# Inverse standard deviation as a power on GpSimd, weight splits on GpSimd alone, the first block normalised tile by tile

## The chip, the cores and the metric

The kernel runs on one core of one Trainium2 chip. The metric is the device time in microseconds of one launch. TensorE (PE in the profile), VectorE (DVE), ScalarE (ACT), GpSimd (POOL) and SyncE (SP) each have an instruction queue of their own and work in the order of that queue.

## The reference

One layer of a transformer-like model: a layernorm, then a time-mixing recurrence and a feed-forward network (FFN) side by side, and a residual sum. x is 4 x 1024 x 512 in float32, HIDDEN is 704, N is 2048.

```python
xn = _layernorm(x, axis=-1)                      # no gain, no bias, eps 1e-5
# attention branch
xx = jnp.concatenate([xn[:, 1:2, :], xn[:, :-1, :]], axis=1) - xn
k = jnp.einsum('btc,hc->bth', xn + xx * time_mix_k, Wk)
r = jnp.einsum('btc,hc->bth', xn + xx * time_mix_r, Wr)
w = jnp.exp(-jnp.exp(time_decay))
# over t: state = state * w + relu(k_t);  o_t = state * r_t
a = jnp.einsum('bth,ch->btc', o, Wv)
a = (a - mean(a)) * rsqrt(var(a) + EPS) * ln_gamma + ln_beta
# ffn branch
D = gelu(float16(xn) @ W0.T + bias0).astype(float16)
E = (D @ W1.T + bias1).astype(float16)
return x + a + E
```

## The kernel before

The 4 x 1024 rows are cut into eight blocks of 512 rows (TB), and a block into four tiles of 128 rows (s = 0 to 3), with the rows in the partitions. The 512 channels make four chunks of 128 (c), the 704 hidden units six chunks (h, the last one of 64), the 2048 inner units of the FFN sixteen (n).

For each block the work is this:

- `layernorm` takes mean and variance of each tile (`stats_of`, L169 and L170, on DVE), makes the inverse standard deviation of all four tiles at once (`rstd_of`: a square root on ACT at L163, a reciprocal on DVE at L164), and normalises each tile in place (`normalize`, L173, on DVE).
- `mixed_inputs` turns the tiles by TensorE transposes (L196) into PSUM tiles `pt`, one per c, from which ACT makes `xnT` in float32 (L199) and `x16` in float16 (L203). DVE forms the shifted difference `xx` (L209) and the two mixed inputs `xk` and `xnT` (L211). POOL saves the last column for the next block (`last`, L206, and L190).
- `attention` makes for each h the product `pk` (L229), its ReLU `rk` on ACT (L237), the recurrence `st` as a scan on DVE (L239), the product `pr` (L251) and `g` = `st` x `pr` on DVE (L258). POOL keeps the last column of `st` as `carry` (L248). `st` has two buffers, `rk` one, and `pk` and `pr` share two PSUM buffers with `pd`.
- `ffn` makes for each n the product `pd` (L300), its GELU in float16 on ACT (L308), a cast `d` back on DVE (L310), and adds the product of `d` with the second weights to four PSUM tiles `pe` (L316). In the text n counts the steps of this loop.
- Between steps of `ffn` other stages are called: at n = 1 `out_stage`, which is `attention_out`; at n = 6 the layernorm of the next block; at n = 10 its `mixed_inputs`. `attention_out` makes `po` (L269), copies it to `z` (L277, ACT), normalises it with its own statistics `mvy` and `ry`, multiplies by gamma and adds beta on POOL (L285, L286), and adds the reloaded x on DVE (L287). The statistics of the next block are `mvx` and `rx`.
- `finish` adds `pe`, the bias and `z` (L337, L338) and stores the tile.

FFN weights are held as two parts that TensorE multiplies one after the other: `split` rounds the loaded tile `raw` to a high part (L121, on ACT) and subtracts it to get a low part (L122, on POOL). W0 is split in sixteen tiles of 128x512 into `w0h` and `w0l`; they are loaded after the attention of block 0 in program order. W1 is split in sixteen tiles in the FFN of block 0, one per n, and written to DRAM (L143), from where the other blocks load it (L145). `raw` has three buffers. All these loads are issued from SP's queue, each once its buffer is free.

The order in which the functions are written is not the order in the queues. A planner orders each engine's instructions by what it thinks is ready, with the program order as priority. So the statistics of the next block are found on DVE directly behind those of `po`, though they are called five steps later.

Of the kernel before, what the change touches and what calls it, by code (L numbers as in the profile page):

```python
# [9 lines left out]
F32 = mybir.dt.float32  # L10
F32R = mybir.dt.float32r
AF = mybir.ActivationFunctionType
ALU = mybir.AluOpType

P = 128
EPS = 1e-5
# [3 lines left out]
def time_mix_and_gelu_ffn(  # L20
# [26 lines left out]
    nc = tc.nc  # L47
# [3 lines left out]
    TB = 512  # L51
    NS = TB // P
    NC = C // P
# [6 lines left out]
    def pool(name, bufs, **kw):  # L60
        return ctx.enter_context(tc.tile_pool(name=name, bufs=bufs, **kw))

    const = pool("const", 1)
    one = pool("one", 1)
    two = pool("two", 2)
    three = pool("three", 3)
    four = pool("four", 4)
    ps_mm = pool("ps_mm", 2, space=bass.MemoryType.PSUM)
    ps_e = pool("ps_e", 4, space=bass.MemoryType.PSUM)
    ps_t = pool("ps_t", 2, space=bass.MemoryType.PSUM)  # L70
    dram = pool("dram", 1, space=bass.MemoryType.DRAM)

    def load_x(i):
        b, t0 = blocks[i]
        tiles = []
        for s in range(NS):
            t = four.tile([P, C], F32, tag="x", name=f"x_{i}_{s}")
            nc.sync.dma_start(t, x[b, t0 + s * P : t0 + (s + 1) * P, :])
            tiles.append(t)
        return tiles  # L80


    x_now = load_x(0)
    ident = const.tile([P, P], F32, name="ident")
    make_identity(nc, ident)
    eps_sb = const.tile([P, 1], F32, name="eps_sb")
    nc.vector.memset(eps_sb, EPS)

    mk_sb = const.tile([P, NC], F32, name="mk_sb")
    mr_sb = const.tile([P, NC], F32, name="mr_sb")  # L90
# [27 lines left out]
    b1_sb = const.tile([P, C], F32, name="b1_sb")  # L118

    def split(hi, lo, raw):  # L120
        nc.scalar.copy(hi, raw)  # L121
        nc.gpsimd.tensor_sub(lo, raw, hi.bitcast(F32))  # L122

    W0G = 512
# [32 lines left out]
    last = const.tile([P, NC, 1], F32, name="last")  # L157
    carry = const.tile([P, NH], F32, name="carry")

    def rstd_of(mv, name):  # L160

        r = two.tile([P, NS], F32, tag="rstd", name=name)
        nc.scalar.activation(r, mv[:, :, 1], AF.Sqrt, bias=eps_sb)  # L163
        nc.vector.reciprocal(r, r)  # L164
        return r

    def stats_of(mv, s, src, name):
        st6 = two.tile([P, 6], F32, tag="st6", name=name)
        nc.vector.bn_stats(st6, src)  # L169
        nc.vector.bn_aggr(mv[:, s, :], st6)  # L170

    def normalize(dst, src, mv, s, rstd):
        nc.vector.tensor_scalar(  # L173
            dst, src, mv[:, s, 0:1], rstd[:, s : s + 1], ALU.subtract, ALU.mult
        )

    def layernorm(i, xs):

        mv = two.tile([P, NS, 2], F32, tag="mv", name=f"mvx_{i}")
        for s in range(NS):  # L180
            stats_of(mv, s, xs[s], f"stx_{i}_{s}")
        rstd = rstd_of(mv, f"rx_{i}")
        for s in range(NS):
            normalize(xs[s], xs[s], mv, s, rstd)

    def mixed_inputs(i, xn):

        t0 = blocks[i][1]
        if t0 > 0:
            nc.gpsimd.tensor_copy(xnT[:, :, 0:1], last)  # L190
        x16s = []
        xk = one.tile([P, NC, TB], F32, tag="xk", name=f"xk_{i}")
        for c in range(NC):
            pt = ps_t.tile([P, TB], F32, tag="pt", name=f"pt_{i}_{c}")
            for s in range(NS):
                nc.tensor.transpose(  # L196
                    pt[:, s * P : (s + 1) * P], xn[s][:, c * P : (c + 1) * P], ident
                )
            nc.scalar.copy(xnT[:, c, 1:], pt)  # L199
            if t0 == 0:  # L200
                nc.vector.tensor_copy(xnT[:, c, 0:1], pt[:, 1:2])
            x16 = four.tile([P, TB], F16, tag="x16", name=f"x16_{i}_{c}")
            nc.scalar.copy(x16, pt)  # L203
            x16s.append(x16)
            if t0 + TB < T:
                nc.gpsimd.tensor_copy(last[:, c, :], xnT[:, c, TB : TB + 1])  # L206
            xx = two.tile([P, TB], F32, tag="xx", name=f"xx_{i}_{c}")
            now = xnT[:, c, 1:]
            nc.vector.tensor_sub(xx, xnT[:, c, :TB], now)  # L209
            for dst, m in ((xk[:, c, :], mk_sb), (now, mr_sb)):  # L210
                nc.vector.scalar_tensor_tensor(  # L211
                    dst, xx, m[:, c : c + 1], now, ALU.mult, ALU.add
                )
        return x16s, xk

    def ffn_input(i, x16s):
        xf = one.tile([P, NC, TB], F32R, tag="xf", name=f"xf_{i}")
        for c in range(NC):
            nc.vector.tensor_copy(xf[:, c, :], x16s[c])
        return xf  # L220

    def attention(i, xk):

        b, t0 = blocks[i]
        g = one.tile([P, NH, TB], F32, tag="g", name=f"g_{i}")
        for h, (h0, hw) in enumerate(hid):
            pk = ps_mm.tile([P, TB], F32, tag="mm", name=f"pk_{i}_{h}")
            for c in range(NC):
                nc.tensor.matmul(  # L229
                    pk[:hw],  # L230
                    wk_sb[c][:, h0 : h0 + hw],
                    xk[:, c, :],
                    start=(c == 0),
                    stop=(c == NC - 1),
                )
            rk = two.tile([P, TB], F32, tag="rk", name=f"rk_{i}_{h}", bufs=1)
            nc.scalar.activation(rk[:hw], pk[:hw], AF.Relu)  # L237
            st = two.tile([P, TB], F32, tag="st", name=f"st_{i}_{h}")
            nc.vector.tensor_tensor_scan(  # L239
                st[:hw],  # L240
                w_sb[:hw, h : h + 1].to_broadcast([hw, TB]),
                rk[:hw],
                0.0 if t0 == 0 else carry[:hw, h : h + 1],
                ALU.mult,
                ALU.add,
            )
            if t0 + TB < T:
                nc.gpsimd.tensor_copy(carry[:hw, h : h + 1], st[:hw, TB - 1 : TB])  # L248
            pr = ps_mm.tile([P, TB], F32, tag="mm", name=f"pr_{i}_{h}")
            for c in range(NC):  # L250
                nc.tensor.matmul(  # L251
                    pr[:hw],
                    wr_sb[c][:, h0 : h0 + hw],
                    xnT[:, c, 1:],
                    start=(c == 0),
                    stop=(c == NC - 1),
                )
            nc.vector.tensor_mul(g[:hw, h, :], st[:hw], pr[:hw])  # L258
        return g

    def attention_out(i, g):

        b, t0 = blocks[i]
        zs = []
        mv = two.tile([P, NS, 2], F32, tag="mv", name=f"mvy_{i}")
        for s in range(NS):
            po = ps_t.tile([P, C], F32, tag="pt", name=f"po_{i}_{s}")
            for h, (h0, hw) in enumerate(hid):
                nc.tensor.matmul(  # L269
                    po,  # L270
                    g[:hw, h, s * P : (s + 1) * P],
                    wv_sb[:hw, h, :],
                    start=(h == 0),
                    stop=(h == NH - 1),
                )
            z = four.tile([P, C], F32, tag="z", name=f"z_{i}_{s}")
            nc.scalar.copy(z, po)  # L277
            stats_of(mv, s, z, f"sty_{i}_{s}")
            zs.append(z)
        rstd = rstd_of(mv, f"ry_{i}")  # L280
        for s in range(NS):
            xr = two.tile([P, C], F32, tag="xres", name=f"xres_{i}_{s}")
            nc.sync.dma_start(xr, x[b, t0 + s * P : t0 + (s + 1) * P, :])
            normalize(zs[s], zs[s], mv, s, rstd)
            nc.gpsimd.tensor_mul(zs[s], zs[s], gamma_sb)  # L285
            nc.gpsimd.tensor_add(zs[s], zs[s], beta_sb)  # L286
            nc.vector.tensor_add(zs[s], xr, zs[s])  # L287
        return zs
# [44 lines left out]
    def finish(i, zs, pe):  # L333
        b, t0 = blocks[i]
        for s in range(NS):
# [2 lines left out]
            nc.vector.tensor_add(zs[s], zs[s], e16)  # L338
            nc.sync.dma_start(out[b, t0 + s * P : t0 + (s + 1) * P, :], zs[s])

    layernorm(0, x_now)
    x16s, xk = mixed_inputs(0, x_now)
    xf = ffn_input(0, x16s)
    for i in range(len(blocks)):
        more = i + 1 < len(blocks)
        state = {}
        g = attention(i, xk)
        if i == 0:
            for grp in range(N // W0G):
                load_w0(grp)  # L350
            load_late_constants()
        if more:
            x_now = load_x(i + 1)

        def out_stage():
            state["zs"] = attention_out(i, g)

        def next_norm():
            layernorm(i + 1, x_now)

        def next_inputs():
            state["mixed"] = mixed_inputs(i + 1, x_now)

        between = {1: out_stage}
        if more:
            between[6] = next_norm
            between[10] = next_inputs
        pe = ffn(i, xf, between)
        if more:
            x16s, xk = state["mixed"]  # L370
            xf = ffn_input(i + 1, x16s)
        finish(i, state["zs"], pe)
# [43 lines left out]
```

## Time and profile before

| | |
|---|---|
| Time, three runs | 1095.02, 1095.55 and 1097.2 us; median 1095.55 |
| The profiled execution | 1094.07 us, of which the span is 1092.1 us |
| Busy: PE, DVE, ACT, POOL | 1026.3, 430.5, 216.5 and 152.8 us |
| Granted TensorE clock, mean | 0.975 of full speed |
| Block 0 | attention from 16.6 us, FFN from 69.5, end about 162.7 |
| Blocks 1 to 6 | 131.4 to 132.0 us each |
| Block 7, with the end | 138 us |

The table gives whole times; what the prediction rests on are rows of the profile. A row of a group gives a line, an engine, an operation, the tile written and the tiles read, and the count; then its busy time and the mean of one in ns; then how long the engine stood idle just before, and what ended the wait. A row of the timeline gives start and duration in us, and the idle time before it in brackets. Busy time of a matmul is modelled, and a matmul at half clock counts as busy.

### The profile page before, as it was taken

The page shows a single profiled execution, that of the slowest core. Times are in us where ns is not written, and L with a number is a line of the kernel's source. Part 1 is how long each engine was busy: PE and PEld are TensorE (multiplying, and loading weights), DVE is VectorE, ACT ScalarE, POOL GpSimd, SP SyncE. Part 2 cuts the span into 40 slices and gives each one's busy share as a digit, 9 for nine tenths or more (in the row PEclk, how much of TensorE's full clock was granted, in tenths as well). Part 3 has the DMA queues.
Part 4 walks back from the last instruction along what each step waited for, and adds up shares of the span by engine and source line. Part 5 has one row for each costly group of instructions (what it writes and reads, how often), then busy time and mean ns, then how long its engine had stood idle before and what let it go on. Part 6 is the DMA issues. An engine that isn't in the chain of part 4 may idle for free.

```text
span 1092.1 us, 8897 instructions
## 1 busy us (share of the span) xinstructions
PE 1026.3 (94%) x3328; PEld 614.0 (56%) x3328; DVE 430.5 (39%) x674; ACT 216.5 (20%) x341; POOL 152.8 (14%) x146
## 2 busy tenths in 40 slices
PE   5899899989999899998999989999899998999997
PEld 2344674447744486445864467544685446744476
DVE  7324453243621625217342163421634225342332
ACT  4312230121201231012310123011230111301211
POOL 3612520031000400004000040000400003000210
PEclk9999899999999899998999989999899998999999
DMA  7730652004600145002540034400443014420043
GB/s 229 247 107 30 208 194 60 19 30 164 205 7 20 58 163 184 1 19 89 171 145 1 20 115 157 133 0 20 135 161 108 1 34 140 131 81 19 20 154 116
DMA packets 43147, 106.37 MB, mean 97 GB/s; under 512 B 8224, under 2 KB 8224, under 8 KB 43104
## 3 DMA queue, kind: packets, MB, share of 16 engines
q1 hardware_dynamic: 39248, 105.79, 29.2%
q10 hardware_dynamic: 3856, 0.02, 0.2%
q8 instruction: 26, 0.43, 0.2%
q14 instruction: 17, 0.14, 0.0%
HBM read 89.01 MB, written 16.78 MB: 97 GB/s over the span
## 4 chain that ended last, share of the span: by engine, by line
PE 54%; issue 31%; DVE 7%; DMA 3%; POOL 3%; ACT 1%; SPq 0%; ACTq 0%; DVEq 0%; POOLq 0%
PE pe L316 19%; PE pd L300 16%; PE pk L229 8%; PE pr L251 6%; PE po L269 4%; DVE z L287 2%; POOL z L285 2%; PE pt L196 1%; DMA out<-z 1%; DVE d L310 1%; DMA w0raw<-in_L_ffn_W 1%; POOL z L286 1%; DVE z L173 1%; POOL w0l L122 1%; DVE e L337 1%
## 5 line engine op out<-in xcount | busy, mean ns | idle before, releaser
L316 PE MATMUL pe<-w,d 128*128 128x512 f32 x1024 | 268.2, 407 | 41.2 <-DVE d L310 41.2
L316 PEld LDWEIGHTS pe<-w,d 128*128 128x128 f32 x1024 | 198.2, 195 | 93.1 <-DVE d L310 47.0
L300 PE MATMUL pd<-xf,w0h 128*128 128x512 f32 x512 | 207.5, 405 | 0.0
L300 PE MATMUL pd<-xf,w0l 128*128 128x512 f32 x512 | 204.1, 399 | 0.0
L229 PE MATMUL pk<-xk,wk 128*128 128x512 f32 (+1 forms) x384 | 177.8, 606 | 4.0 <-ACT rk L237 3.9
L269 PE MATMUL po<-wv_sb,g 128*128 128x512 f32 (+1 forms) x384 | 177.2, 607 | 0.0
L251 PE MATMUL pr<-xnT,wr 128*128 128x512 f32 (+1 forms) x384 | 174.4, 595 | 1.2 <-DVE g L258 0.9
L308 ACT ACTIVATE d<-pd,b_sb 128x512 f16<-128x512 f32 x128 | 88.3, 690 | 344.6 <-PE pd L300 340.0
L310 DVE CAST d<-d 128x512 fp32r<-128x512 f16 x128 | 64.3, 504 | 224.8 <-ACT d L308 224.3
L285 POOL TENSOR_TENSOR z<-z,gamma_sb 128x512 f32<-128x512 f32 x32 | 50.8, 1606 | 545.6 <-DVE z L173 545.6
L269 PEld LDWEIGHTS po<-wv_sb,g 128*128 128x128 f32 (+1 forms) x384 | 68.2, 189 | 104.0 <-issue 103.2
L229 PEld LDWEIGHTS pk<-xk,wk 128*128 128x128 f32 (+1 forms) x384 | 70.2, 185 | 100.3 <-issue 93.6
L251 PEld LDWEIGHTS pr<-xnT,wr 128*128 128x128 f32 (+1 forms) x384 | 69.4, 181 | 98.6 <-issue 94.7
L300 PEld LDWEIGHTS pd<-xf,w0h 128*128 128x128 f32 x512 | 98.2, 192 | 34.3 <-issue 12.6
L300 PEld LDWEIGHTS pd<-xf,w0l 128*128 128x128 f32 x512 | 97.8, 191 | 22.4
L169 DVE BATCH_NORM_STATS2 sty<-z 128x6 f32<-128x512 f32 x32 | 22.2, 695 | 164.4 <-ACT z L277 164.4
L237 ACT ACTIVATE rk<-pk 128x512 f32<-128x512 f32 (+1 forms) x48 | 28.6, 596 | 280.2 <-PE pk L229 280.2
L239 DVE TENSOR_TENSOR_SCAN st<-w_sb,rk 128x512 f32<-128x512 f32 (+1 forms) x24 | 31.4, 1308 | 77.4 <-ACT rk L237 77.4
L258 DVE TENSOR_TENSOR g<-st,pr 128x512 f32<-128x512 f32 (+1 forms) x48 | 32.9, 686 | 68.5 <-PE pr L251 68.2
L239 DVE TENSOR_TENSOR_SCAN st<-w_sb,carry,rk 128x512 f32<-128x512 f32 (+1 forms) x24 | 30.8, 1283 | 70.2 <-ACT rk L237 70.2
L277 ACT COPY z<-po 128x512 f32<-128x512 f32 x32 | 18.8, 586 | 168.3 <-PE po L269 168.3
L286 POOL TENSOR_TENSOR z<-z,beta_sb 128x512 f32<-128x512 f32 x32 | 44.6, 1414 | 0.0
(41 smaller groups left out, 449.7 us busy)
## 6 DMA issues: line engine op xcount, KB each, us to landing
w<-w1d SPq DMA_DIRECT2D x112, 512.0 KB, 3.3
x<-in_L_attn_x SPq DMA_DIRECT2D x32, 256.0 KB, 3.9
xres<-in_L_attn_x SPq DMA_DIRECT2D x32, 256.0 KB, 2.7
w1d<-w SPq DMA_DIRECT2D x16, 512.0 KB, 2.9
out<-z SPq DMA_DIRECT2D x32, 256.0 KB, 4.4
w0raw<-in_L_ffn_W SPq DMA_DIRECT2D x16, 256.0 KB, 3.7
w1raw<-in_L_ffn_W SPq DMA_DIRECT2D x16, 256.0 KB, 3.5
wk<-in_L_attn_Wk SPq DMA_DIRECT2D x4, 352.0 KB, 4.5
```

The source lines that it names most:

```text
L229: nc.tensor.matmul(pk[:hw], wk_sb[c][:, h0 : h0 + hw], xk[:, c, :], start=(c == 0), stop=(c == NC - 1),)
L237: nc.scalar.activation(rk[:hw], pk[:hw], AF.Relu)
L239: nc.vector.tensor_tensor_scan(st[:hw], w_sb[:hw, h : h + 1].to_broadcast([hw, TB]), rk[:hw], 0.0 if t0 == 0 else carry[:hw, h : h + 1], A ...
L251: nc.tensor.matmul(pr[:hw], wr_sb[c][:, h0 : h0 + hw], xnT[:, c, 1:], start=(c == 0), stop=(c == NC - 1),)
L258: nc.vector.tensor_mul(g[:hw, h, :], st[:hw], pr[:hw])
L269: nc.tensor.matmul(po, g[:hw, h, s * P : (s + 1) * P], wv_sb[:hw, h, :], start=(h == 0), stop=(h == NH - 1),)
L285: nc.gpsimd.tensor_mul(zs[s], zs[s], gamma_sb)
L286: nc.gpsimd.tensor_add(zs[s], zs[s], beta_sb)
L300: nc.tensor.matmul(pd, w[c][:, cols], xf[:, c, :], start=(c == 0 and w is w0h), stop=(c == NC - 1 and w is w0l),)
L308: nc.scalar.activation(d16, pd, AF.Gelu, bias=b0_sb[:, n : n + 1])
L310: nc.vector.tensor_copy(d, d16)
L316: nc.tensor.matmul(pe[s], d[:, s * P : (s + 1) * P], w1[:, part, :], start=(n == 0 and part == 0), stop=(n == NN - 1 and part == 1),)
```

## The change

It has four parts.

- `rstd_of` now works on POOL: it adds eps to the variance and raises the sum to the power -0.5 with a constant tile `nhalf`. The square root on ACT and the reciprocal on DVE are gone, and with them the constant `eps_sb`. This holds for the layernorm of each block and for that of `po`.
- `split` makes both parts on POOL; the rounding copy was on ACT.
- The first block goes tile by tile: statistics, `rstd_of` for a single column, normalise, and four transposes, before the next tile. It uses four PSUM tiles of the pool that `pe` has later. The other blocks keep the old order (`transposed`).
- `mixed_inputs` takes the transposed tiles as an argument.

```diff
-    eps_sb = const.tile([P, 1], F32, name="eps_sb")
-    nc.vector.memset(eps_sb, EPS)
+    nhalf = const.tile([P, NS], F32, name="nhalf")
+    nc.vector.memset(nhalf, -0.5)
...
     def split(hi, lo, raw):
-        nc.scalar.copy(hi, raw)
+        nc.gpsimd.tensor_copy(hi, raw)
         nc.gpsimd.tensor_sub(lo, raw, hi.bitcast(F32))
...
-    def rstd_of(mv, name):
+    def rstd_of(var, name):
-        r = two.tile([P, NS], F32, tag="rstd", name=name)
-        nc.scalar.activation(r, mv[:, :, 1], AF.Sqrt, bias=eps_sb)
-        nc.vector.reciprocal(r, r)
+        n = var.shape[1]
+        r = two.tile([P, n], F32, tag=f"rstd{n}", name=name)
+        nc.gpsimd.tensor_scalar_add(r, var, EPS)
+        nc.gpsimd.tensor_tensor(r, r, nhalf[:, :n], ALU.pow)
         return r
...
+    def first_transposed(xs):
+        pts = [ps_e.tile([P, TB], F32, tag="pe", name=f"pt_0_{c}") for c in range(NC)]
+        for s in range(NS):
+            mv = four.tile([P, 1, 2], F32, tag="mv0", name=f"mvx_0_{s}")
+            stats_of(mv, 0, xs[s], f"stx_0_{s}")
+            rstd = rstd_of(mv[:, :, 1], f"rx_0_{s}")
+            normalize(xs[s], xs[s], mv[:, 0, 0:1], rstd)
+            for c in range(NC):
+                nc.tensor.transpose(
+                    pts[c][:, s * P : (s + 1) * P], xs[s][:, c * P : (c + 1) * P], ident
+                )
+        return pts
...
-    layernorm(0, x_now)
-    x16s, xk = mixed_inputs(0, x_now)
+    x16s, xk = mixed_inputs(0, first_transposed(x_now))
```

More of the change, by code (lines that the diff above doesn't have):

```diff
@@ L170, in stats_of, with normalize @@
         nc.vector.bn_aggr(mv[:, s, :], st6)
[L172 to L175, printed above, removed]
+    def normalize(dst, src, mean, rstd):
+        nc.vector.tensor_scalar(dst, src, mean, rstd, ALU.subtract, ALU.mult)
     def layernorm(i, xs):
@@ L181, in layernorm, with transposed @@
             stats_of(mv, s, xs[s], f"stx_{i}_{s}")
-        rstd = rstd_of(mv, f"rx_{i}")
+        rstd = rstd_of(mv[:, :, 1], f"rx_{i}")
         for s in range(NS):
[L184 to L192, printed above, removed]
+            normalize(xs[s], xs[s], mv[:, s, 0:1], rstd[:, s : s + 1])
+    def transposed(i, xn):
         for c in range(NC):
@@ L198, in mixed_inputs @@
                 )
+            yield pt
+    def first_transposed(xs):
[10 more added lines that the diff above has]
+        return pts
+    def mixed_inputs(i, pts):
+        t0 = blocks[i][1]
+        if t0 > 0:
+            nc.gpsimd.tensor_copy(xnT[:, :, 0:1], last)
+        x16s = []
+        xk = one.tile([P, NC, TB], F32, tag="xk", name=f"xk_{i}")
+        for c, pt in enumerate(pts):
             nc.scalar.copy(xnT[:, c, 1:], pt)
@@ L279, in attention_out @@
             zs.append(z)
-        rstd = rstd_of(mv, f"ry_{i}")
+        rstd = rstd_of(mv[:, :, 1], f"ry_{i}")
         for s in range(NS):
@@ L283, in attention_out @@
             nc.sync.dma_start(xr, x[b, t0 + s * P : t0 + (s + 1) * P, :])
-            normalize(zs[s], zs[s], mv, s, rstd)
+            normalize(zs[s], zs[s], mv[:, s, 0:1], rstd[:, s : s + 1])
             nc.gpsimd.tensor_mul(zs[s], zs[s], gamma_sb)
@@ L361, in next_inputs @@
         def next_inputs():
-            state["mixed"] = mixed_inputs(i + 1, x_now)
+            state["mixed"] = mixed_inputs(i + 1, transposed(i + 1, x_now))
         between = {1: out_stage}
```

## The prediction

> **What bounds the kernel now.** The first view read is the page: busy time by engine, then the groups of instructions with what ended the idle time before them.
>
> ```profile
> PE 1026.3 (94%) x3328; PEld 614.0 (56%) x3328; DVE 430.5 (39%) x674; ACT 216.5 (20%) x341; POOL 152.8 (14%) x146
> ...
> L316 PE MATMUL pe<-w,d 128*128 128x512 f32 x1024 | 268.2, 407 | 41.2 <-DVE d L310 41.2
> ```
>
> TensorE is the bound, and GpSimd is idle for 86% of the span. What can be won is TensorE's idle time: of 65.8 us, 41.2 us stand before the second FFN product (L316) and end with VectorE's cast of `d` (L310). 11.4 us are the start, before the first transpose. The busy time also hides stretches at half speed: eight matmuls of L316 take 1.84 us at full rate.
>
> The timeline of block 1 (start, duration, then idle before) shows one of these stalls; the same order of DVE instructions, with 5.10 us of TensorE idle, stands in each of blocks 1 to 6, and with 6.23 us (and one cast of `x` more) in block 0.
>
> ```profile
> 233.93 0.17 DVE L170 BATCH_NORM_AGGREGATE mvy<-sty 128x2 f32<-128x6 f32 x1
> ...
> 234.17 0.69 ACT L308 ACTIVATE d<-pd,b_sb 128x512 f16<-128x512 f32 x1 [1.48 <-PE pd L300]
> 234.88 1.28 ACT L163 ACT_TABLE_LOAD   x1
> 236.18 0.30 ACT L163 ACTIVATE ry<-mvy,eps_sb 128x4 f32<-128x4 f32 x1
> 236.51 0.18 DVE L164 RECIPROCAL ry<-ry 128x4 f32<-128x4 f32 x1
> 236.74 3.87 DVE L173 TENSOR_SCALAR z<-z,mvy,ry 128x512 f32<-128x512 f32 x4
> ...
> 237.35 2.97 POOL L285 TENSOR_TENSOR z<-z,gamma_sb 128x512 f32<-128x512 f32 x2 [81.59 <-DVE z L173]
> ...
> 241.79 3.40 DVE L287 TENSOR_TENSOR z<-xres,z 128x512 f32<-128x512 f32 x2 [1.10 <-POOL z L286]
> 245.12 1.48 DVE L310 CAST d<-d 128x512 fp32r<-128x512 f16 x1
> 246.65 3.41 PE L316 MATMUL pe<-w,d 128*128 128x512 f32 x8 [5.10 <-DVE d L310]
> ```
>
> The cast that TensorE needs had its input at 239.90 (a GELU of 239.21 + 0.69). It runs only at 245.12, since two L287 adds stand ahead of it in DVE's queue, and these wait for POOL's multiply and add (2.97 + 1.4 us), which wait for the normalised z, which waits for `ry`. From the end of `mvy` (234.10) to the first normalise (236.74) pass 2.64 us: ACT was inside a GELU, then loaded a table.
>
> A second stall is in block 0's attention, again in the timeline:
>
> ```profile
> 45.76 0.62 ACT L121 CAST w0h<-w0raw 128x512 fp32r<-128x512 f32 x1 [0.65 <-DMA w0raw<-in_L_ffn_W]
> 49.20 0.62 ACT L121 CAST w0h<-w0raw 128x512 fp32r<-128x512 f32 x1 [2.83 <-DMA w0raw<-in_L_ffn_W]
> 51.18 0.62 ACT L121 CAST w<-w1raw 128x512 fp32r<-128x512 f32 x1 [1.36 <-DMA w1raw<-in_L_ffn_W]
> 51.71 0.59 ACT L237 ACTIVATE rk<-pk 128x512 f32<-128x512 f32 x1
> 52.35 6.67 PE L229 MATMUL pk<-xk,wk 128*128 128x512 f32 x8 [3.88 <-ACT rk L237]
> ```
>
> The `pk` that this ReLU empties was done at 45.0, but the ReLU stood behind casts that waited for DMA. TensorE lost 3.9 us idle and then ran eight matmuls in 6.67 us, where steady blocks need 3.43.
>
> And the start, in the same view:
>
> ```profile
> 8.89 1.28 ACT L163 ACT_TABLE_LOAD   x1
> 8.90 0.18 DVE L170 BATCH_NORM_AGGREGATE mvx<-stx 128x2 f32<-128x6 f32 x1
> 10.19 0.30 ACT L163 ACTIVATE rx<-mvx,eps_sb 128x4 f32<-128x4 f32 x1
> 10.52 0.18 DVE L164 RECIPROCAL rx<-rx 128x4 f32<-128x4 f32 x1 [1.44 <-ACT rx L163]
> ```
>
> All four x tiles wait for the last one's statistics (9.08), then for the root, until 10.73.
>
> **What the Trainium skill says.** "ScalarE: Activation LUTs", What ACT_TABLE_LOAD costs: a load takes about 1283 ns and about as much again of drain. The trace agrees on 1283 ns (19 loads in all); the drain is not seen, the activation starts 0.02 us after. "SBUF — State Buffer", SBUF: two separate sides: VectorE and GpSimd lock one pair of ports for a whole instruction, and the loser waits. The trace agrees: a normalise is 0.53 us alone and up to 1.52 us beside POOL, a cast of `d` 0.43 and 1.48. "TensorE: Matmul & The Clock Gate", Part 1: after an idle window of about 3.4 us the clock is halved. The trace agrees: after 5.10 us idle eight matmuls take 3.4 to 3.8 us instead of 1.84, after 1.82 us idle (block 7) 2.1. No page prices a power on GpSimd.
>
> **The change, part by part.**
>
> *Root out, power in.* Gone: 16 roots, 16 reciprocals and, by the order of functions left (exponential once, then GELU), 17 of the 19 table loads. ACT is 20% busy, so their sum (17 x 1.28 us) counts only where it stands in the chain above. Added on POOL: an add and a power, 19 times each (15 of 128x4, four of 128x1). The add: between 0.18 us (POOL's copy of 128x1) and 0.60 (its copy of 128x4, next to DVE work); I take 0.40. The power is in no row. Floor: 0.18 us, as any small POOL instruction. Ceiling: 1.26 us, what POOL takes for a 512-column subtraction; in four columns that would allow (1.26 - 0.18) / 4 = 270 ns a column against 2.1 ns for a subtraction. Nothing excludes more, and that is a rival below. I take 0.5 us. With two hops of 0.07 us (normalise end to POOL start in the trace) the new latency is 0.14 + 0.40 + 0.50 = 1.04 us instead of 2.64: the chain to L287 starts **1.6 us earlier**. POOL had been idle for 81.6 us, so nothing is ahead of `ry`. But `rx` of the next block issues its add and power in the same stretch, 0.9 us, and if they come ahead of the z adds, these are late by that; I charge half, 0.45. Net 1.15 us per block. The stall is then about 4 us, and the half-speed stretch after it (about 1.9 us in L316, up to 0.9 more in L300) may or may not come; I credit 0.8. So 1.95 us for each of blocks 1 to 6: **-11.7 us**. That the GELU of `d` needs no table load is worth nothing by itself: it was ready 5.2 us before its cast.
>
> Block 7 has no next norm; its table was loaded before `mvy` came and the latency is only 0.91 us (1029.54 to 1030.45). There the change costs about 0.1 us.
>
> *Splits on POOL alone.* 32 casts of 0.62 us leave ACT, 32 one-input copies of 128x512 come to POOL. "GPSIMD Engine Reference", 4.1 Engine selection, puts one-input work at roughly line rate and two-input work at twice VectorE's time. The trace has only the two-input one (1.26 us alone). Floor: half of it, 0.63; ceiling: 1.26. I take 0.65. A split is then 1.9 us of POOL, 16 of them 31 us. Before, the 16 took 18.5 to 51.2, 2.0 us each, paced by three `raw` buffers; so the stream keeps its pace and begins up to 2.5 us earlier, as it no longer waits for ACT's copies of block 0 (issued at 9.44, landed 6.6 later, first cast at 18.50). ACT's queue no longer holds a DMA wait, so each ReLU runs when `pk` is done. What TensorE lost to it: 0.9 (the late `g` at 29.8) + 0.3 + 4.0 + 3.2 (slow clock) = 8.4 us; check: after 26.2, ten groups of 3.43 us would end at 60.5, they ended at 69.5, so 8.9. I take **-8.5 us**. What is late next: POOL's queue now holds the DMA waits, and behind them the `carry` copies (L248); the scan two steps later needs them (two `st` buffers), a slack of 13.7 us. The `last` copies (L206) have no such slack but were issued ahead of the first split. w1 of step 0, split at about 57, is needed at about 64. SP's order stays, its waits for `raw` now end on POOL.
>
> Against that: POOL locks DVE's port for 32 x 0.65 us more in block 0. In attention DVE is half idle (24.8 of 52.9 us busy), but in out_stage and at the inputs of block 1 (1.47 us of stall) it isn't. In block 0's out_stage a w1 split of 1.9 us instead of 1.3 stands in the z chain too. I charge **+1.5 us** for both, and count no gain from that stage.
>
> *First block tile by tile.* Three tiles are normalised and transposed while the next is loaded; the last has its statistics at 9.08, its rstd 0.9 us later, 0.53 us for the normalise, four transposes. DVE's chain of L209 and L211 can start at about 12.2 instead of 13.84. But that chain (2.2 us per c, four of them) is what paces the first matmuls until 26, and POOL's splits, begun earlier, lock its port earlier. From -1.6 to +1 us; I take **-0.8**.
>
> Sum: -11.7 + 0.1 - 8.5 + 1.5 - 0.8 = **-19.4 us**. The profiled execution took 1094.07 us (span 1092.1 and 2.0 around it), 1.5 below the median of 1095.55. 1094.07 - 19.4 = 1074.7, on the median 1076.2. **Forecast 1076 us**.
>
> **The rivals.**
>
> *The planner's order flips* (0.15). It orders DVE's queue by when it thinks things are ready. If one cast of `d`, 1.28 us earlier without its table load, comes ahead of the L287 adds, the stall goes, as nearly in block 7, where a cast stands between and 1.82 + 1.04 us are lost. Then 6 x (5.1 + 2.2 of slow clock - 1) = 38 us instead of 11.7: about 1050. Against it: the z chain comes earlier as well, by about as much.
>
> *The power is slow* (0.22), the case on the other side. Its time P counts in eight out_stages and once at the start. Leaving out the clock's 4.8 us, the sum is -14.6 + 9 x (P - 0.5): **above 2.1 us the kernel is slower than before**; at 5 us it is +26, or 1121. `rx` on the same queue could add to that. For it: nothing in the trace shows such an operation. Against it: four columns only.
>
> *POOL becomes block 0's bound* (0.15): a copy near 1.26 us makes a split 2.5 us, 40 us for 16, and w1 comes late for the first steps; DVE waits at the port. Then block 0 gives nothing or costs 5, and the power's gain remains: 1083 to 1098, about 1090. That the change doesn't do what it says can only be that half: the wait for DMA moves from ACT's queue into POOL's.
>
> **How the numbers follow.** The forecast has 0.48, with its own range 1066 to 1087 (power from 0.18 to 1.26 us, clock recovered or not). The range of 8 in 10 must reach down to the flipped order and up into the slow power to P of about 3: 1046 to 1104. A measurement tells about 0.2%, 2.2 us, from no change. Faster: nearly all of the forecast, the flip, two thirds of the third rival: 0.72. Slower: the slow power and a little more: 0.22. Same: 0.06.
>
> **What would show it.** Right: two table loads; `ry` about 1 us after `mvy`; TensorE idle before L316 of about 4 us per block instead of 5.1; no wait of L229 for `rk` in block 0, and its attention ending near 60. Wrong: a power of over 2 us, POOL busy without gaps up to L285, L229 or L239 waiting for `carry`, or a cast of `d` standing ahead of L287.

## The result, and the profile after

**No measurable difference.** After: 1095.89 us (median; 1095.56 to 1097.4). Before, on the same chip: 1095.28 us. The ratio is 1.0006, with a 95% interval of 0.9989 to 1.0024. The forecast of 1076 us was wrong by 20 us. The profiled execution took 1095.56 us (span 1093.8), against 1094.07 (span 1092.1) before.

The page of the kernel after, busy time by engine and the group of the second FFN product (line 316 before is line 335 now):

```profile
PE 1026.1 (94%) x3328; PEld 612.6 (56%) x3328; DVE 427.0 (39%) x658; ACT 171.1 (16%) x276; POOL 202.0 (18%) x216
...
L335 PE MATMUL pe<-w,d 128*128 128x512 f32 x1024 | 268.8, 408 | 44.9 <-DVE d L329 44.9
```

ACT lost 45 us of work and POOL took on 49. TensorE's busy time is unchanged, and its idle time before the second product did not fall from 41.2 us to some 34 (six blocks by the forecast's 1.15 us each): it rose to 44.9, and the rise is that of block 0 (from 7.7 to 12.1).

The timeline of block 1 after (start, duration, then idle before) shows how:

```profile
236.52 0.17 DVE L171 BATCH_NORM_AGGREGATE mvy<-sty 128x2 f32<-128x6 f32 x1
...
236.75 0.69 ACT L327 ACTIVATE d<-pd,b_sb 128x512 f16<-128x512 f32 x1 [1.47 <-PE pd L319]
236.77 0.23 POOL L164 TENSOR_SCALAR ry<-mvy 128x4 f32<-128x4 f32 x1 [78.47 <-DVE mvy L171]
237.08 1.04 POOL L165 TENSOR_TENSOR ry<-ry,nhalf 128x4 f32<-128x4 f32 x1
238.15 3.83 DVE L174 TENSOR_SCALAR z<-z,mvy,ry 128x512 f32<-128x512 f32 x4 [0.74 <-POOL ry L165]
...
241.91 1.48 DVE L329 CAST d<-d 128x512 fp32r<-128x512 f16 x1
243.31 3.44 DVE L306 TENSOR_TENSOR z<-xres,z 128x512 f32<-128x512 f32 x2
...
243.44 3.46 PE L335 MATMUL pe<-w,d 128*128 128x512 f32 x8 [3.01 <-DVE d L329]
...
248.88 0.18 DVE L171 BATCH_NORM_AGGREGATE mvx<-stx 128x2 f32<-128x6 f32 x1
...
250.53 0.68 POOL L164 TENSOR_SCALAR rx<-mvx 128x4 f32<-128x4 f32 x1
...
251.29 1.04 POOL L165 TENSOR_TENSOR rx<-rx,nhalf 128x4 f32<-128x4 f32 x1
252.37 0.55 DVE L174 TENSOR_SCALAR x<-x,mvx,rx 128x512 f32<-128x512 f32 x1 [1.24 <-POOL rx L165]
252.83 0.68 DVE L306 TENSOR_TENSOR z<-xres,z 128x512 f32<-128x512 f32 x1
253.43 0.54 DVE L174 TENSOR_SCALAR x<-x,mvx,rx 128x512 f32<-128x512 f32 x1
253.88 0.42 DVE L329 CAST d<-d 128x512 fp32r<-128x512 f16 x1
...
254.36 2.12 PE L335 MATMUL pe<-w,d 128*128 128x512 f32 x8 [1.67 <-DVE d L329]
```

Read it from the statistics down. `mvy` ends at 236.69, the first normalise starts at 238.15: 1.46 us where it was 2.64, so the power does shorten that step. But the order of DVE's queue is another one. Before, the cast of `d` of step 2 ran inside the wait for the root, and so did the statistics of the next block's x:

```profile
234.90 0.43 DVE L310 CAST d<-d 128x512 fp32r<-128x512 f16 x1
...
236.60 0.22 DVE L170 BATCH_NORM_AGGREGATE mvx<-stx 128x2 f32<-128x6 f32 x2
```

Now the cast stands **behind** all four normalises of z: its input is ready at 237.44, it starts at 241.91, and TensorE idles 3.01 us. On the chip it would have fitted into the wait, since DVE stood idle until 238.15. The planner orders by what it thinks, ahead of time. The cast of step 3, which cost the old 5.10 us, is no longer the problem. A second stall has come instead. The statistics of x stand behind z's normalises and adds on DVE and end only at 249.06, 12.4 us behind `mvy` (before: 2.7 us behind it). The add and the power of `rx` come behind eight z operations on POOL, so the add starts at 250.53. DVE stands 1.24 us at the first x normalise, and the cast of `d` of step 4 is queued behind that, another L306 and the next x normalise. The old 5.10 us became 3.01 + 1.67 in blocks 1, 3 and 5, 3.01 + 0.82 + 2.14 in blocks 2 and 6, and 3.01 + 0.48 in block 4.

Blocks 1 to 6 take 794.5 us together instead of 795.9. In the profile before they take 131.7 to 133.2 us each, and block 7 with the end 133.5; the 131.4 to 132.0 and 138 us in the table of the section on the time before don't agree with its trace.

Block 0's attention did gain. The timeline after, in the stretch where the ReLU of L237 had stood behind casts that waited for DMA:

```profile
46.69 0.61 POOL L121 CAST w0h<-w0raw 128x512 fp32r<-128x512 f32 x1 [0.17 <-DMA w0raw<-in_L_ffn_W]
46.84 0.60 ACT L256 ACTIVATE rk<-pk 128x512 f32<-128x512 f32 x1 [6.27 <-PE pk L248]
...
50.07 3.60 PE L248 MATMUL pk<-xk,wk 128*128 128x512 f32 x8
```

The ReLU waits for `pk` and for nothing else, and eight matmuls take 3.60 us instead of 6.67. The attention of block 0 runs from 15.5 to 64.0 us (before: 16.6 to 69.4). But block 0 as a whole ends at 165.4 instead of 162.8: 5.4 us won, 8.0 given back in its FFN. The timeline of that place:

```profile
107.78 1.07 POOL L121 CAST w<-w1raw 128x512 fp32r<-128x512 f32 x1
108.94 1.28 POOL L122 TENSOR_TENSOR w<-w1raw,w 128x512 fp32r<-128x512 f32 x1
...
110.74 0.23 POOL L164 TENSOR_SCALAR rx<-mvx 128x4 f32<-128x4 f32 x1
110.94 1.26 POOL L122 TENSOR_TENSOR w<-w1raw,w 128x512 fp32r<-128x512 f32 x1
112.16 1.05 POOL L165 TENSOR_TENSOR rx<-rx,nhalf 128x4 f32<-128x4 f32 x1
...
113.24 0.81 DVE L174 TENSOR_SCALAR x<-x,mvx,rx 128x512 f32<-128x512 f32 x1 [4.86 <-POOL rx L165]
...
116.66 3.75 PE L335 MATMUL pe<-w,d 128*128 128x512 f32 x8 [6.78 <-DVE d L329]
```

The power of `rx` stands on POOL behind z work and two splits of W1; DVE stands 4.86 us at the x normalise, with a cast of `d` behind it, and TensorE idles 6.78 us, where it idled 6.23 before. Besides, the cast of step 2 behind z costs 3.12 us here too, and a stall of 1.47 us at the end of the block has become 2.16. So 4.4 of the 8.0 us are idle time. The rest is busy time: the same matmuls of this FFN take 89.3 us instead of 85.7, since more of them run at the slow clock.

### The profile page after: what moved, and what is told of

Same layout as the page of the kernel before. It is cut to its first block, busy times and chain, and to the rows that moved or that the text cites. A ratio compares the mean times of both kernels' runs of the same rounds, so it can differ in the third digit from the quotient of the medians.

```text
span 1093.8 us, 8867 instructions
## 1 busy us (share of the span) xinstructions
PE 1026.1 (94%) x3328; PEld 612.6 (56%) x3328; DVE 427.0 (39%) x658; ACT 171.1 (16%) x276; POOL 202.0 (18%) x216
## 4 chain that ended last, share of the span: by engine, by line
PE 81%; POOL 8%; DVE 6%; issue 2%; DMA 1%; ACT 1%; DVEq 0%; POOLq 0%; ACTq 0%
PE pe L335 18%; PE pd L319 16%; PE po L288 16%; PE pr L270 15%; PE pk L248 15%; POOL z L304 3%; POOL z L305 2%; DVE z L306 1%; PE pt L190 1%; POOL ry L165 1%; DVE x L174 1%; DVE xx L228 1%; POOL rx L165 1%; DVE z L174 1%; DVE d L329 1%
## 5 line engine op out<-in xcount | busy, mean ns | idle before, releaser
L335 PE MATMUL pe<-w,d 128*128 128x512 f32 x1024 | 268.8, 408 | 44.9 <-DVE d L329 44.9
L335 PEld LDWEIGHTS pe<-w,d 128*128 128x128 f32 x1024 | 196.9, 194 | 99.3 <-DVE d L329 41.2
L248 PE MATMUL pk<-xk,wk 128*128 128x512 f32 (+1 forms) x384 | 174.7, 597 | 3.8 <-DVE xk L230 3.8
L329 DVE CAST d<-d 128x512 fp32r<-128x512 f16 x128 | 66.7, 523 | 223.7 <-ACT d L327 223.7
L306 DVE TENSOR_TENSOR z<-xres,z 128x512 f32<-128x512 f32 x32 | 48.2, 1527 | 3.2 <-POOL z L305 3.2
```

Source lines behind the costliest of these rows:

```text
L248: nc.tensor.matmul(pk[:hw], wk_sb[c][:, h0 : h0 + hw], xk[:, c, :], start=(c == 0), stop=(c == NC - 1),)
L329: nc.vector.tensor_copy(d, d16)
L335: nc.tensor.matmul(pe[s], d[:, s * P : (s + 1) * P], w1[:, part, :], start=(n == 0 and part == 0), stop=(n == NN - 1 and part == 1),)
```

## The experiments

The theory to test: the time is set by what stands ahead of a cast of `d` in DVE's queue, and by which of those instructions waits for POOL. The change moved these waits and removed none. The rivals: the power or POOL's splits cost by themselves what the change wins elsewhere; the tile-by-tile start costs; the clock takes it. The last is out: the granted clock was 0.976 to 0.981 in the runs after, against 0.975 in the profile before, and TensorE's busy time is the same.

### One part of the change alone

**Splits on POOL alone** (in the kernel before):

```diff
     def split(hi, lo, raw):
-        nc.scalar.copy(hi, raw)
+        nc.gpsimd.tensor_copy(hi, raw)
```

> The kernel before with one edit: the high part of each weight split is copied on POOL. Theory Q (the order of the queues decides: ReLU no longer waits behind DMA waits on ACT, and no power stands behind the splits on POOL): block 0's attention ends about 5 us earlier (near 64 instead of 69.5), its out_stage stall stays near 6.2 us, blocks 1 to 7 are unchanged: -5 us, between -3 and -8. Rival P (POOL becomes block 0's bound and locks DVE's port, which ate the gain): block 0 gains nothing, 0 to +2 us.

Measured: 1095.17 us against 1097.02, ratio 0.9984 (0.9977 to 0.9991). A gain of 1.85 us, below what was expected (3 to 8). Attention ends 3.7 us earlier (65.7), but block 0 only 1.0 earlier (161.8): a new stall of 1.93 us stands in its FFN.

**The power alone** (in the kernel before):

```diff
-        nc.scalar.activation(r, mv[:, :, 1], AF.Sqrt, bias=eps_sb)
-        nc.vector.reciprocal(r, r)
+        nc.gpsimd.tensor_scalar_add(r, mv[:, :, 1], EPS)
+        nc.gpsimd.tensor_tensor(r, r, nhalf, ALU.pow)
```

> The kernel before with one edit: rstd_of by add and power on POOL, for all blocks. Theory Q: ry comes 1.2 us earlier, but the four z normalises move ahead of the cast of d of step 2, and the next x normalises wait on DVE for an rx whose power stands behind eight z operations on POOL, with a cast of d behind them: two stalls of about 3.0 and 1.7 us per block instead of one of 5.1, so no gain: -2 to +3 us in all. Rival L (the earlier ry shortens the old stall by its latency gain of 1.2 us, and the loss comes from the splits): -7 to -11 us.

Measured: 1097.15 us, ratio 1.0000 (0.9988 to 1.0011), as expected. Blocks 1 to 6 show the stalls of the kernel after, 3.04 us and one or two more of 0.4 to 2.2; block 0 has 3.05 and 3.84. So the change of order comes from the power alone.

**The tile-by-tile start alone** (the kernel after, with the root and the rounding copy back on ACT):

> The kernel before with one edit: the first block is normalised and transposed tile by tile; root on ACT, splits on ACT as before. Both theories: DVE's chain of L209 and L211 paces the start, so 0, between -1.5 and +1 us.

Measured: 1098.88 us, ratio 1.0017 (1.0010 to 1.0025), 1.9 us slower, which is outside what was expected. The first `pk` starts at 17.9 us (16.6 before): ACT loads a table five times by 13.0 us, since roots and exponentials alternate, and the last two roots wait for that (before: twice by 10.2). With the power alone `pk` starts at 16.8, with both parts at 15.5, so they only pay together. The three parts alone sum to +0.1 us (-1.85 + 0.13 + 1.86); the whole change measured +0.6.

### What stands in the queues

**`rx` off POOL** (the kernel after; the rstd of x of blocks 1 to 7 is again a root on ACT and a reciprocal, that of z stays a power):

```diff
-        rstd = rstd_of(mv[:, :, 1], f"rx_{i}")
+        rstd = rstd_of(mv[:, :, 1], f"rx_{i}", root=True)
```

> The changed kernel with one edit: the rstd of the next block's x (blocks 1 to 7) is again a square root on ACT and a reciprocal on DVE; ry stays a power on POOL. Theory Q: the x normalises no longer wait for POOL; the second stall (1.7 us in blocks 1 to 6, 6.8 in block 0) goes or shrinks to under 1: 8 to 15 us under the changed kernel, 1081 to 1088. Rival P: the stalls are POOL's port, so they stay: within 3 us of the changed kernel, 1093 to 1098.

Measured: 1088.83 us, ratio 0.9927 (0.9904 to 0.9951), just over what was expected. The first stall stays (3.02 us), the second shrinks to between 0.3 and 1.5 us in five of blocks 1 to 6 (the other has 0.84 + 1.94), and block 0's from 6.78 to 4.10. Where `rx` is made is worth some 8 us.

**The x normalises behind casts of `d`** (the kernel after; each of the four is queued behind the latest cast, in steps 7 to 10, instead of all at step 6):

```diff
-        for s in range(NS):
-            normalize(xs[s], xs[s], mv[:, s, 0:1], rstd[:, s : s + 1])
+        return lambda s: normalize(xs[s], xs[s], mv[:, s, 0:1], rstd[:, s : s + 1])
...
+                with tc.issue_after(casts[-1].ins):
+                    state["norm"](s)
...
+                between[s + 7] = norm_tile(s)
```

> The changed kernel; the four x normalises are queued on DVE behind the casts of d of steps 7 to 10, one behind each, and nothing else is moved. Theory Q (a cast of d stands behind an x normalise that waits for rx, whose power stands behind the z work on POOL): the second stall (about 1.7 us in blocks 1 to 6, 6.8 in block 0) goes, the first one (3.0 us, with a half-speed stretch) stays: 8 to 16 us under the changed kernel, 1080 to 1088. Rival P (ports, or POOL's total work): within 3 us of the changed kernel.

Measured: 1072.63 us, ratio 0.9778 (0.9754 to 0.9803), better than expected. `rx` is computed on POOL as before; only what waits for it has moved behind the casts, and block 0's stall of 6.78 us has become 0.95. One stall of 3.0 us is left in each of blocks 1 to 7 (2.55 in the last), and block 0 ends at 156.1.

**The forecast's own order** (the previous kernel, and the tail of z, too, is queued behind the cast of step 2):

```diff
-        between = {1: out_stage}
+        between = {1: out_stage, 2: out_tail}
...
+        def out_tail():
+            with tc.issue_after(casts[-1].ins):
+                state["tail"]()
```

> As the one before, and in addition the z normalises are queued behind the cast of d of step 2: the order of the kernel before, with the x normalises out of the way. This is the world that the forecast assumed. Theory Q: one stall per block again, in front of step 3, with two L306 adds ahead of its cast, of 5.1 us less the latency gain of about 1.2: 3.9 us and a half-speed stretch; about 1 us per block worse than the one before: 1087 to 1096. Rival (the cast of step 2 behind z is the whole loss): as good as or better than the one before.

Measured: 1085.44 us, ratio 0.9896 (0.9878 to 0.9914), a little better than expected. The timeline of block 1 of this kernel:

```profile
231.24 0.43 DVE L333 CAST d<-d 128x512 fp32r<-128x512 f16 x1
231.92 3.87 DVE L174 TENSOR_SCALAR z<-z,mvy,ry 128x512 f32<-128x512 f32 x4 [0.25 <-POOL ry L165]
...
236.97 3.43 DVE L307 TENSOR_TENSOR z<-xres,z 128x512 f32<-128x512 f32 x2 [0.51 <-POOL z L306]
...
240.31 1.48 DVE L333 CAST d<-d 128x512 fp32r<-128x512 f16 x1
...
241.85 3.78 PE L339 MATMUL pe<-w,d 128*128 128x512 f32 x8 [3.92 <-DVE d L333]
```

This is the order that the prediction took for granted: a cast in the wait for `ry`, then z, then two adds, then the late cast. The stall is 3.92 us in each of blocks 1 to 6: 5.10 less the 1.18 us by which `ry` comes earlier. So the forecast's mechanism is real, in a queue that the changed kernel doesn't have.

### The order pinned, with and without the change

The kernel after, with the z tail spread over the steps as well: normalise of tile s behind the cast of step 2 + s, the residual add at step 5 + s, the next block's statistics at step 5, its normalise of tile s at step 6 + s.

```diff
+        def step(n):
+            def stage():
+                with tc.issue_after(casts[-1].ins):
+                    if 2 <= n < 2 + NS:
+                        state["scale"](n - 2)
+                    if n == 5 and more:
+                        state["norm"] = layernorm(i + 1, x_now)
+                    if 6 <= n < 6 + NS and more:
+                        state["norm"](n - 6)
+                    if 5 <= n < 5 + NS:
+                        state["residual"](n - 5)
...
```

> The changed kernel with its DVE queue laid out by hand: each z normalise behind a cast of d (steps 2 to 5), each L306 add three steps later (5 to 8), the next block's statistics behind step 5, each x normalise behind steps 6 to 9. Theory Q: no cast of d waits for POOL any more, so nearly all of the 44.9 us of idle before L335 and the half-speed stretches behind it go: 1040 to 1055. Rival P (ports and POOL's work as such): still over 1075.

Measured: 1038.52 us, ratio 0.9473 (0.9451 to 0.9495), a little better than expected. The page, and the timeline of block 1 of this kernel:

```profile
PE 1007.1 (97%) x3328; PEld 603.3 (58%) x3328; DVE 380.8 (37%) x658; ACT 171.1 (17%) x276; POOL 194.9 (19%) x216
...
L340 PE MATMUL pe<-w,d 128*128 128x512 f32 x1024 | 257.7, 396 | 4.9 <-DVE d L334 4.6
```

```profile
230.60 0.43 DVE L334 CAST d<-d 128x512 fp32r<-128x512 f16 x1 [2.67 <-ACT d L332]
230.94 0.54 DVE L174 TENSOR_SCALAR z<-z,mvy,ry 128x512 f32<-128x512 f32 x1
...
233.40 2.02 PE L340 MATMUL pe<-w,d 128*128 128x512 f32 x8
234.32 0.43 DVE L334 CAST d<-d 128x512 fp32r<-128x512 f16 x1 [2.84 <-ACT d L332]
```

Each cast waits only for its GELU, and one normalise follows it. The idle time before the second product is 4.9 us instead of 44.9, all of it in block 0; blocks 1 to 6 take 125.1 to 125.3 us. The span is 57.9 us shorter than that of the kernel after (1035.9 against 1093.8): 40.0 us less idle time before the second product, and 19.0 us less busy time of TensorE, as fewer matmuls run at the slow clock (its mean granted clock is 0.996 instead of 0.981); other waits grew by 1.1.

The layout moves more than the casts. POOL's work on z and the reloads of x move with it, and instructions of DVE that ran beside POOL's are shorter now: a residual add takes 0.79 us on average instead of 1.53, and DVE is busy for 380.8 us instead of 427.0. How much of the gain is the place of the casts, and how much the shorter instructions, the runs don't separate.

The kernel **before**, in the same layout:

> The kernel before (root on ACT, splits with the copy on ACT, first block as before) with the same layout of the DVE queue by hand. Theory Q: the stalls go here too, so the power is worth nothing beside the order; only the ReLU waits of block 0's attention remain: 3 to 10 us over the one before, 1046 to 1062. Rival L (the power's shorter latency and the table loads that it saves are what matters): 15 us or more over it.

Measured: 1038.91 us, ratio 0.9474 (0.9455 to 0.9493): 0.4 us over the pinned kernel after, where 3 to 10 were expected. Its table loads, 33 of them (19 in the kernel before), don't show. Blocks 1 to 6 take 125.0 to 125.2 us. The line that answers, from its page:

```profile
L321 PE MATMUL pe<-w,d 128*128 128x512 f32 x1024 | 256.0, 394 | 3.1 <-DVE d L315 3.1
```

With the order pinned, the whole change is worth nothing that these times can tell; the order, with all that the layout moves, is worth 5.3%, with it or without it. In the two profiled executions alone, the change gains 7.4 us by the end of block 0's attention (63.98 against 71.35) and gives 3.7 back in its FFN (90.8 us against 87.1). Single executions differ, too: the attention of block 0 takes 54.8 us in the pinned kernel before and 52.8 in the profile of the kernel before, though the layout changes nothing in it.

### Single costs in the pinned order

These four ran on another chip, on which the kernel before took 1097.27 us instead of 1096.87.

**The power three times** (the pinned kernel after, with two more powers into a scratch tile for each rstd):

```diff
+        for k in range(2):
+            q = two.tile([P, n], F32, tag=f"idle{n}", name=f"{name}_q{k}", bufs=1)
+            nc.gpsimd.tensor_tensor(q, r, nhalf[:, :n], ALU.pow)
         nc.gpsimd.tensor_tensor(r, r, nhalf[:, :n], ALU.pow)
```

> The changed kernel with the DVE queue laid out by hand, and two further powers into a scratch tile ahead of each power (about 2.1 us more of POOL and of latency for each rstd of four columns, 1.1 for one column). Theory Q: in this layout no cast of d waits for an rstd, so the power's price is hidden in blocks 1 to 7; only the start pays, 1 to 4 us: 1039 to 1043. Rival L (the latency of the rstd is on the path): 8 out_stages x 2.1 us and the start: 1055 to 1060.

Measured: 1046.69 us, ratio 0.9541 (0.9525 to 0.9557); between the expectations. Of the span's 7.9 us over the pinned kernel after, 2.7 are at the start (first `pk` at 18.2 instead of 15.4), 4.4 in the rest of block 0, where `rx` again stands behind POOL's W1 splits (one stall of 6.91 us), and 0.8 in all that follows: blocks 1 to 6 take 125.2 to 125.5 us. So where no cast stands behind it, two more powers, some 2 us of latency, cost the steady blocks 0.16 us each: the latency of rstd hardly counts there.

**W1's rounding copy back on ACT, W0's on POOL**, first in the pinned kernel after:

```diff
-            split(w1[:, 0, :], w1[:, 1, :], raw)
+            split(w1[:, 0, :], w1[:, 1, :], raw, nc.scalar.copy)
```

> The changed kernel with the DVE queue laid out by hand, and the high part of W1's splits back on ACT, W0's on POOL. Theory Q: the ReLUs of block 0 stay free of most DMA waits, and POOL has 16 copies less in block 0's FFN, which took about 91 us there against 87 with the copies on ACT: 1 to 4 us under the layout with all splits on POOL (1038.5). Rival: a ReLU now waits behind the first W1 casts: no gain, 0 to +3.

Measured: 1046.31 us, ratio 0.9537 (0.9523 to 0.9551). Worse than all on POOL, against both expectations. The timeline, in block 0's attention:

```profile
57.06 1.25 ACT L121 CAST w<-w1raw 128x512 fp32r<-128x512 f32 x2 [14.94 <-DMA w1raw<-in_L_ffn_W]
58.22 0.59 ACT L255 ACTIVATE rk<-pk 128x512 f32<-128x512 f32 x1
...
58.86 6.03 PE L247 MATMUL pk<-xk,wk 128*128 128x512 f32 x8 [7.07 <-ACT rk L255]
```

Two W1 casts suffice: ACT waits for their DMA with a ReLU behind them, and TensorE loses 7.07 us idle and 2.4 to its clock (6.03 us where such matmuls take 3.60). Attention ends at 75.3 instead of 64.0; the FFN gets 3.1 back.

The same split of work in the pinned kernel before:

> The kernel before (root on ACT, first block as before) with the DVE queue laid out by hand and only W0's high parts copied on POOL. Theory Q: equal to the changed kernel with the same layout and the same splits, within 2 us, since root or power is hidden: 1034 to 1039. Rival L: 5 us or more over it.

Measured: 1043.98 us, ratio 0.9515 (0.9501 to 0.9529); the same stall, 6.54 us, and slower than expected for it. It is 2.3 us faster than the run with the change (1046.31), and the slowest of its runs (1044.18) is faster than the fastest with the change (1045.92): with the copies shared like this the change costs. By the traces 1.1 us of it is there at the end of block 0 (162.0 against 163.1).

**Four buffers for the single-column rstd of the start** (on the mixed-copy version of the pinned kernel after, `bufs=4`):

> As the layout with W0's splits on POOL, with four buffers instead of two for the rstd. In the start of the changed kernel the third tile's add waited 2.6 us for a buffer that the first normalise frees. Theory: the last normalise comes 1 us earlier, and the chain of L228 and L230 after it too: -0.5 to -1.5 us. Rival: POOL's splits lock DVE's port in that chain anyway: 0.

Measured: 1047.14 us, ratio 0.9545 (0.9530 to 0.9559); no gain. In the kernel after, the third tile's add had waited 2.59 us for such a buffer. With four that wait is gone, but the order flips once more, now on POOL: all four adds stand ahead of the first power, so no power runs before the last tile's statistics end at 9.21. The first normalise starts at 10.09 us instead of 9.29, and the first `pk` at 16.1 instead of 15.4. So this run doesn't show what the buffer alone is worth.

## Why the prediction was wrong

**The sum's main term, -11.7 us in blocks 1 to 6, measured -1.4.** Three things stood in it.

- *The order.* The step was "the chain to L287 starts 1.6 us earlier", with DVE's order as before. This failed. The order did flip, but not as the rival of that name had it: no cast moved ahead of the adds at no cost; one moved behind the normalises and another behind an x normalise that waits for POOL. The prediction listed "a cast of `d` standing ahead of L287" as a sign of error, and that is what the trace shows at 241.91. Another of its signs, a scan waiting for `carry`, came as well (3.63 us of DVE at 61.46), but TensorE didn't wait for it.
- *`rx` on POOL.* It was charged 0.45 us, as work ahead of z. Its real cost is as a wait: its statistics end 12.4 us behind `mvy` instead of 2.7, it stands behind eight z operations on POOL (in block 1 from 249.06 to 250.53), and ahead of a cast of `d` on DVE. Taking it off POOL alone gave some 8 us.
- *The clock credit* of 0.8 us per block. In the forecast's own order eight matmuls after the 3.92 us of idle still take 3.52 to 3.78 us. In that order blocks 1 to 6 gained 8.1 us (787.8 instead of 795.9), of which 6 x 1.18 = 7.1 are idle time. (The prediction's 1.84 us for eight matmuls at full rate is eight times their distance from start to start; the rows, which run to the end of the last, have 2.00 to 2.02.)

**The latency** was 1.46 us, not 1.04. The groups of the kernel after, by form (count, then busy and mean in ns):

```profile
L165 POOL TENSOR_TENSOR ry<-ry,nhalf 128x4 f32<-128x4 f32 x8 | 8.3, 1038 | 0.7
L165 POOL TENSOR_TENSOR rx<-rx,nhalf 128x1 f32<-128x1 f32 x4 | 2.4, 610 | 0.2
L164 POOL TENSOR_SCALAR ry<-mvy 128x4 f32<-128x4 f32 x8 | 1.8, 229 | 544.9 <-DVE mvy L171 544.9
...
L121 POOL CAST w<-w1raw 128x512 fp32r<-128x512 f32 x16 | 10.3, 645 | 31.4 <-PE pe L335 31.4
```

The power is 1.04 us where 0.5 was taken; the add is 0.23 alone (0.61 for `rx`, beside DVE work) where 0.40 was. The power and the add of `ry` lie inside the bounds given, the add of `rx` at their upper end, and the power is far below the 2.1 us from which the rival "the power is slow" was to decide.

**Splits, -8.5 + 1.5, measured: attention -4.3 (48.5 us instead of 52.8), block 0's FFN +8.0.** The mechanism was right: no wait for `rk` is left, and the copy takes 0.65 us for W1, as taken (0.91 for W0, beside DVE's work). Two terms were mis-sized. The port: beside POOL's splits DVE's chain for the first products is longer (two L228 take 2.77 us, where two L209 took 1.29), and TensorE waits 2.09, 0.55 and 1.89 us for DVE, where it waited 0.37 and 0.86. So the first full group of eight `pk` matmuls starts at 27.30 instead of 26.20, and attention ends at 64.0, not near 60. The Trainium skill's page "SBUF — State Buffer", SBUF: two separate sides, names a lock on a port that the two engines share; these times agree with it, though no run shows the lock itself. And the charge for block 0's FFN was 1.5 us, for DVE's port and a slower z chain. The power alone costs 4.5 us there (97.9 against 93.4), POOL's splits alone 2.7 (96.1), so the 8.0 are nearly their sum; the largest stall, at `rx`, is 3.84 us with the power alone and 6.78 with W1's splits on POOL as well.

**The start, -0.8, measured -1.1** (first `pk` at 15.5 instead of 16.6). Near in size by luck. The step was that three tiles are normalised while the next is loaded, so that DVE's chain starts earlier. The timeline after:

```profile
9.19 0.18 DVE L171 BATCH_NORM_AGGREGATE mvx<-stx 128x2 f32<-128x6 f32 x1
9.29 0.97 DVE L174 TENSOR_SCALAR x<-x,mvx,rx 128x512 f32<-128x512 f32 x2
...
12.03 0.55 DVE L174 TENSOR_SCALAR x<-x,mvx,rx 128x512 f32<-128x512 f32 x1 [0.46 <-POOL rx L165]
...
13.96 0.69 DVE L228 TENSOR_TENSOR xx<-xnT 128x512 f32<-128x512 f32 x1
```

No tile is normalised ahead of the last one's statistics, and DVE's chain starts at 13.96, where it started at 14.03. What let `pk` start earlier is TensorE's queue: the transposes, in four PSUM tiles, are over by 13.75, where the second half of them started at 14.83 and stood ahead of `pk`. By the first full group, at 27.30 instead of 26.20, that gain is lost again.

**What was right:** two table loads are left, ACT's load was worth nothing in itself (the pinned kernel before has 33 and is no slower), and the rival "flip" had the right price for a stall with its slow clock. It put these at 5.1 + 2.2 = 7.3 us per block; pinning the order took 7.6 from each of blocks 1 to 6 of the kernel before ((795.9 - 750.5) / 6). The order was worth more than everything the forecast summed up, and the prediction gave a flip a chance only in its good form, not in its bad one. The Trainium skill's page "PSUM — Partial Sum Buffer", Engine vs sequencer instructions, states that VectorE's queue is strictly first in, first out. The trace agrees: a cast ready at 237.44 waited 4.47 us behind four normalises.

What stays open: what the planner reckons when it puts that cast behind the normalises. The runs show its orders, not its reasons. Open, too, is how the gain of the pinned order divides between the casts' places and DVE's shorter instructions, and what would pace the start with both the buffers and the order of tiles kept.

## What to carry to other kernels

When a planner orders a queue, an edit that shortens one latency can reorder the queue, and the order may be worth more than the latency: look at which instruction that the bounding engine needs stands behind one that waits for another engine. Before pricing such an edit, pin the order (here: one normalise behind each cast) in both kernels and compare; here both fell by 5.3%, and the edit was then worth nothing measurable. Moving a small operation to an idle engine is not free when that engine's queue holds bulk work or a DMA wait ahead of it: it was `rx` behind W1's splits on GpSimd, and a ReLU behind W1's casts on ScalarE.

## What the runs showed of the hardware

- A power on GpSimd takes 1.04 us for 128x4 and 0.61 us (mean) for 128x1: by an estimate from these two, about half a microsecond is fixed and a column adds some 0.14 us ((1.04 - 0.61) / 3).
- GpSimd's rounding copy of 128x512 takes 0.61 us at its fastest; W0's sixteen, beside VectorE's work in block 0's attention, take 0.91 us on average and up to 1.54.
- With no idle ahead, eight matmuls of 512 columns take 2.02 us, after 1.67 us of idle 2.12. After 5.10 us (six blocks of the kernel before) they take 3.41 to 3.78. After 3.0 us it varies: in blocks 1 to 6 of the kernel after they take 3.46, 2.12, 2.69, 3.78, 3.46 and 2.12 us. The Trainium skill's page "TensorE: Matmul & The Clock Gate", Part 1, names a window of about 3.4 us of idle; here 3.0 us, counted from ends of matmuls that the profile models, cost as much as 5.1 in one block and nothing in two.
